# An embedding-attention kernel whose single-row fetches are dealt out anew between ScalarE and SyncE

## The chip, the core and the metric

The kernel runs on one NeuronCore of a Trainium2 chip. Its metric is device microseconds (us) of one execution, the median of three: 16508.57 us before the change (16477.51 to 16532.16). The hardware profiler recorded one execution; its record runs from the first to the last instruction and is called the span.

The engines are named as the profile names them: PE (TensorE, matmuls), PEld (its weight loads), DVE (VectorE), ACT (ScalarE), POOL (GpSimd), SP (SyncE). ACT, SP and POOL also issue DMAs. Each engine works through its own list of instructions in order.

## The reference

The reference scores 16384 users. Each has 69 item numbers and a label; all 70 are looked up in a table of 100001 rows of 96 floats. The 69 looked-up rows pass through a small attention network (one hidden layer of 64), are weighted, summed into 10 groups, and go with the label's row through a top network (200, 80, 1).

```python
u  = emb[batch_user]                    # 16384 x 69 x 96
ql = emb[batch_label[:, 0]]
z  = concatenate([q, u, q - u, q * u])  # q: ql repeated over the 69 fields
h  = _dice(z @ W1 + b1, a1)             # (a*(1-p)+p)*x with p = sigmoid(x)
att = (h @ W2 + b2) @ W3 + b3
pre = where(batch_user < 100000, u * att, 0)
pooled = einsum('gf,bfe->bge', window, pre)
x = concatenate([pooled, ql])
# two dice layers (200, 80), then one output
```

## The kernel before

**Tiling.** 16384 x 69 lookups are 2208 chunks of 512 rows; a chunk is four gathers of 128 rows. Two chunks make a step, so there are 1104 steps. A block is 512 users: 69 chunks, or 34.5 steps; there are 32 blocks. Of a block's 69 chunks, 64 hold eight users with 64 fields each, and the last five hold one field of all 512 users. These five (the tail chunks) take other matmuls, at L396, L401 and L423.

**A step.** `fetch(i)` gathers eight tiles of 128 rows into `u` (POOL, L266), turns each by a PE transpose into `ptr` (L325), and DVE copies it and multiplies it by the label's row (L376, L379). Two steps later `hidden` does the attention layer: PE's matmuls into `ph` (L396 to L403), then on ACT the sigmoid (L405) and, on its result, a scaled identity (L406), and on DVE the product with `ph` (L407): this is the gate. Every fourth step PE turns four gated results into attention scores (`prow`, L414), which ACT copies out (`row`, L416) and DVE spreads into weights (`rw`, L436). Seven steps after the fetch `pool` sums the weighted rows (PE `acc`, L325; DVE, L470). Once per block come the label's gather and its preparation (L348 on PE, copied by ACT at L349) and the top network in ten pieces, with three pairs of activations on ACT (L483, L484).

**Singles.** Some of the 8832 gathers of `u` are not done by POOL. For the chunks that stand in the tables `SP_CHUNKS` and `ACT_CHUNKS` the fourth tile of 128 rows is fetched row by row, by 128 DMAs of 384 bytes (L301) issued from SP or from ACT into a ring of buffers. PE then waits for a semaphore and reads the ring in place of `u`. The byte offset of each row is read from SBUF into a register; one load (L286) brings 32 of them. SP fetches whole tiles; one is needed every 5.5 steps, the table being `2 * (int(5.5 * s) + 6) + 1`. ACT fetches 20 rows in each step, right behind the step's two activations, so a tile takes 6.4 steps; it is needed two steps after its last row. SP's ring has 8 buffers, ACT's 4.

**Order.** The order of the work is written out by hand: a table `plan` has a list of pieces for each step, and the program is emitted step by step. What an engine does when follows from this order and from semaphores alone. The buffers set how far engines may drift apart: `u` has 15 buffers, `ph` 2, `ptr` 2, `acc` 1, `y` 6.

Of the kernel before, what the change touches and what calls it, by code (L numbers as in the profile page):

```python
# [18 lines left out]
P = 128  # L19
# [29 lines left out]

ROW_BYTES = 4 * E  # L50
SLOT = 3
SP_CHUNKS = [2 * (int(5.5 * s) + 6) + 1 for s in range(199)]
SP_RING = 8
ACT_ROWS = 20
ACT_CHUNKS = [2 * ((s + 1) * P // ACT_ROWS + 2) for s in range(170)]
ACT_RING = 4
SINGLES = SP_CHUNKS + ACT_CHUNKS
NSB = (len(SINGLES) + P - 1) // P
NSEM = 8
# [3 lines left out]
def chunk_of(c):  # L63

    n, k = divmod(c, NCH)
    if n == NBLK - 1 and k >= EARLY:
        k = NMAIN + k - EARLY if k < EARLY + NTAIL else k - NTAIL
    return n, k
# [47 lines left out]
def rec_kernel(  # L116
# [269 lines left out]
                nc.vector.tensor_tensor(quT[:, j, :], ptr, q[:, 0:BLK], ALU.mult)  # L386
        return u, uT, quT

    def hidden(i, uT, quT):

        ph = ps_h.tile([P, 512], F32, tag="h", name=f"ph{i}")
        places = [chunk_of(2 * i + j) for j in range(2)]
        sums = [ph[j * H1 : (j + 1) * H1, :] for j in range(2)]
        for (n, k), p in zip(places, sums):
            if k >= NMAIN:
                nc.tensor.matmul(p, Cq, qTs[n % 2], start=True, stop=False)  # L396
        for j, ((n, k), p) in enumerate(zip(places, sums)):
            if k < NMAIN:
                nc.tensor.matmul(p, As[n % 2][:, k // 4, :], uT[j], start=True, stop=False)  # L399
            else:  # L400
                nc.tensor.matmul(p, A, uT[j][0:E], start=False, stop=False)  # L401
        for j, p in enumerate(sums):
            nc.tensor.matmul(p, Wp, quT[:, j, :], start=False, stop=True)  # L403
        y = ypool.tile([P, 512], F32, tag="y", name=f"y{i}")
        nc.scalar.activation(y, ph, AF.Sigmoid, scale=S_DICE)  # L405
        nc.scalar.activation(y, y, AF.Identity, bias=a1c, scale=na1c)  # L406
        nc.vector.tensor_mul(y, ph, y)  # L407
        return y
# [131 lines left out]
    pooled, pres, x1s, x2s, qs, us, hs, ys, bands, rws, p1s = ({} for _ in range(11))  # L540
# [17 lines left out]
    def rows_of(b, n):  # L558
        return lambda: attend_rows(b, n)

    def spread_of(b, n):
        return lambda: spread(b, n)

    def pool_of(k):
        return lambda: pool(k)

    def hidden_of(k):
        return lambda: ys.__setitem__(k, hidden(k, *hs[k]))

    def tails_of(k):  # L570
        def work():
            uT = hs.pop(k)[0]
            for j in range(2):
                if chunk_of(2 * k + j)[1] >= NMAIN:
                    attend_tail(k, j, ys[k], uT)

        return work

    def fetch_of(k, between=()):
        def work():  # L580
            for j in range(2):
                n = chunk_of(2 * k + j)[0]
                if n not in pooled:
                    pooled[n] = bpool.tile([E, G, BLK], F32, tag="pooled", name=f"pooled{n}")
                    pres[n] = xpool.tile([E, NTAIL, BLK], F32, tag="pre", name=f"pre{n}")
            u, uT, quT = fetch(k, lambda: [w() for w in between])
            us[k], hs[k] = u, (uT, quT)

        return work
# [4 lines left out]
    def at(step, *work):  # L594
        plan.setdefault(step, []).extend(work)

    by_sync = Singles("sp", nc.sync, mybir.EngineType.SP, SP_CHUNKS, 0, range(SP_RING), 32)
    for s, m in enumerate(SP_CHUNKS):
        at(max(0, m // 2 - 6), lambda s=s: by_sync.fetch(s, 0, P))

    by_scalar = Singles(
        "act",
# [1 line left out]
        mybir.EngineType.Activation,  # L604
        ACT_CHUNKS,
        len(SP_CHUNKS),
        range(SP_RING, SP_RING + ACT_RING),
        32,
    )
    def scalar_rows(i):  # L610

        row, stop = i * ACT_ROWS, min((i + 1) * ACT_ROWS, len(ACT_CHUNKS) * P)
        while row < stop:
            s, start = divmod(row, P)
            n = min(P - start, stop - row)
            by_scalar.fetch(s, start, start + n)
            row += n

    c = NPAIR - CLOSE
    for i in range(c):  # L620
        if i >= 3 and (i - 3) % 4 == 3:
            at(i, rows_of(i - 6, 4))
        if i >= 3:
            at(i, tails_of(i - 3))
        if i >= 4 and (i - 4) % 4 == 3:
            at(i, spread_of(i - 7, 4))
        if i >= 2:
            at(i, hidden_of(i - 2))
        at(i, lambda i=i: scalar_rows(i))
        if i < c - CLOSE:  # L630
            if i >= POOL_LAG:
                at(i, pool_of(i - POOL_LAG))
        else:

            for k in {0: (-15, -14), 1: (-13,), 3: (-12, -11), 4: (-10, -9), 7: (-8, -7)}.get(i - c + 8, ()):
                at(i, pool_of(c + k))
        at(i, fetch_of(i))

    at(c, pool_of(c - 6), pool_of(c - 5), tails_of(c - 3), hidden_of(c - 2), fetch_of(c))
    at(c + 1, tails_of(c - 2), hidden_of(c - 1), fetch_of(c + 1))  # L640
    at(c + 2, rows_of(c - 4, 4), tails_of(c - 1), hidden_of(c), spread_of(c - 4, 4), pool_of(c - 4), fetch_of(c + 2))
    at(c + 3, pool_of(c - 3), pool_of(c - 2), hidden_of(c + 1), fetch_of(c + 3, [hidden_of(c + 2)]))
# [5 lines left out]
    for n in range(NBLK):  # L648
        first, end = n * NCH // 2, ((n + 1) * NCH - 1) // 2
# [104 lines left out]
```

## Time and profile before

| what | value |
|---|---|
| median of three runs | 16508.57 us |
| span of the profiled execution | 10780.4 us |
| time of the profiled execution itself | not shown; the span lies 5728.2 us below the median of the runs |
| gathers by POOL | 8463 of `u`, 128 of labels |
| rows issued singly by SP and by ACT | 25472 (199 tiles) and 21760 (170 tiles) |
| mean granted PE clock | 0.749 of full speed |

In the groups of instructions, a row reads: line, engine, operation, output<-inputs, shapes, count | busy us, mean ns of one | idle us just before them and what ended it. DMA-issuing instructions on SP and ACT do not count as busy: they stand in the timeline as ACTq and SPq, where a row's second number is the time from the first to the end of the last of a run of equal instructions. An ACT that is idle in the groups may therefore be issuing rows. The record says nothing of what lies outside its first and last instruction.

### The profile page before, as it was taken

Reading aid. Unit: us, or ns where it says so; the run is one execution under the profiler, and the core shown is the slowest. Engines: PE = TensorE matmul, PEld = TensorE weight load, DVE = VectorE, ACT = ScalarE, POOL = GpSimd, SP = SyncE. Lnnn points to the kernel's source line nnn. Section 1 sums busy time; section 2 is a strip of 40 time slices with the busy share of each in tenths; the row PEclk is TensorE's granted clock in tenths of the full one; section 3 lists DMA queues with packets and bytes.
Section 4 is the critical chain, followed back from the end, with each engine's and each line's share of the span. In section 5 each row is a group of like instructions: output and inputs, shape, how many; then the busy total and the mean of one; then the engine's idle time right before and its main releaser. Section 6 shows DMA issues by size and latency. Waiting matters only on the chain.

```text
span 10780.4 us, 204439 instructions
## 1 busy us (share of the span) xinstructions
PE 8756.9 (81%) x41797; PEld 4310.8 (40%) x41797; DVE 4235.1 (39%) x7535; ACT 1884.4 (17%) x2761; POOL 8110.8 (75%) x8597
## 2 busy tenths in 40 slices
PE   6888888888887788877888788888887887888888
PEld 3434444434433344433433344333343343443335
DVE  4333333333333333333333343333333334333333
ACT  1111111111111111111111111111111111111112
POOL 7777777777777777777777777777777777777776
PEclk7777777677777777777777777777777777777778
DMA  2222222222222222222222222222222222222221
GB/s 50 42 42 42 45 42 42 42 42 45 42 42 42 45 42 42 42 42 45 42 42 42 42 44 42 42 42 42 44 42 42 42 42 44 42 42 42 42 42 34
DMA packets 372495, 460.70 MB, mean 43 GB/s; under 512 B 232114, under 2 KB 232626, under 8 KB 371106
## 3 DMA queue, kind: packets, MB, share of 16 engines
q0 software_dynamic: 274912, 422.81, 18.9%
q1 hardware_dynamic: 52802, 16.36, 1.0%
q10 hardware_dynamic: 43520, 8.44, 0.7%
q14 instruction: 925, 7.58, 0.2%
q8 instruction: 336, 5.51, 0.2%
HBM read 446.81 MB, written 0.07 MB: 41 GB/s over the span
## 4 chain that ended last, share of the span: by engine, by line
POOL 40%; PE 21%; issue 19%; DMA 12%; ACTq 6%; ACT 2%; DVE 1%; POOLq 0%
POOL u L266 40%; DMA u<-in_rows,ids 12%; ACTq L301 4%; PE acc L325 4%; PE p L502 4%; PE ph L399 3%; PE ph L403 3%; PE ptr L325 2%; PE prow L414 1%; ACTq L286 1%; PE pa L423 1%; ACT y L405 1%; POOL q L266 1%; PE ph L396 1%; PE ph L401 1%
## 5 line engine op out<-in xcount | busy, mean ns | idle before, releaser
L266 POOL DMA_INDIRECT u<-in_rows,ids x8463 | 7989.1, 944 | 2583.5 <-issue 2389.6
L325 PE MATMUL ptr<-ident,u 128*96 128x128 f32 x8463 | 1925.1, 332 | 1606.1 <-DMA u<-in_rows,ids 1555.6
L407 DVE TENSOR_TENSOR y<-ph,y 128x512 f32<-128x512 f32 x1104 | 763.5, 692 | 4972.6 <-ACT y L406 4699.0
L325 PEld LDWEIGHTS acc<-rw,u 128*96 128x96 f32 x15702 | 1674.4, 188 | 1332.5 <-issue 840.4
L325 PEld LDWEIGHTS ptr<-ident,u 128*96 128x96 f32 x8463 | 1131.6, 151 | 2282.7 <-DMA u<-in_rows,ids 1853.2
L325 PE MATMUL acc<-rw,u 128*96 128x20 f32 x15702 | 1792.0, 259 | 212.0 <-DVE rw L436 177.6
L376 DVE COPY uT<-ptr 96x512 f32<-96x512 f32 x2208 | 1489.0, 674 | 739.9 <-PE ptr L325 737.5
L405 ACT ACTIVATE y<-ph 128x512 f32<-128x512 f32 x1104 | 658.8, 597 | 6119.1 <-PE ph L403 3304.1
L399 PE MATMUL ph<-uT,A 128*64 128x512 f32 x4096 | 1598.9, 856 | 0.0
L403 PE MATMUL ph<-quT,wn 96*64 96x512 f32 x4416 | 1540.5, 767 | 0.0
L379 DVE TENSOR_TENSOR quT<-ptr,qT 96x512 f32<-96x512 f32 x2048 | 1379.1, 673 | 0.0
L406 ACT ACTIVATE y<-y,wn,na1c 128x512 f32<-128x512 f32 x1104 | 897.9, 813 | 36.6
L403 PEld LDWEIGHTS ph<-quT,wn 96*64 96x64 f32 x4416 | 429.4, 183 | 1002.5 <-issue 1001.8
L502 PE MATMUL p<-pooled,wf 96*100 96x512 f32 (+1 forms) x1400 | 667.7, 624 | 0.0
L414 PE MATMUL prow<-y,v 128*32 128x512 f32 x2208 | 507.2, 885 | 65.4 <-DVE y L407 57.6
L399 PEld LDWEIGHTS ph<-uT,A 128*64 128x64 f32 x4096 | 259.6, 172 | 609.6 <-issue 605.5
L416 ACT COPY row<-prow 128x512 f32<-128x512 f32 (+1 forms) x277 | 161.6, 583 | 1733.2 <-issue 675.0
L470 DVE COPY pooled<-acc 96x160 f32<-96x160 f32 x1008 | 420.5, 417 | 99.1 <-PE acc L325 97.6
L502 PE MATMUL p<-pre,V 96*100 96x512 f32 (+1 forms) x700 | 398.0, 714 | 11.1 <-DVE x L485 10.8
L502 PEld LDWEIGHTS p<-pooled,wf 96*100 96x100 f32 x1400 | 249.6, 190 | 316.5 <-issue 316.5
L436 DVE SCALAR_TENSOR_TENSOR rw<-patt,bb,wn 128x320 f32<-128x320 f32 x554 | 276.1, 539 | 116.8 <-PE patt L431 114.7
L485 DVE SCALAR_TENSOR_TENSOR x<-p,wf,g 100x512 f32<-100x512 f32 (+3 forms) x105 | 73.9, 704 | 523.6 <-ACT g L484 523.5
(72 smaller groups left out, 2706.1 us busy)
## 6 DMA issues: line engine op xcount, KB each, us to landing
ring<-in_rows SPq DMA_DIRECT2D x25472, 0.4 KB
ring<-in_rows ACTq DMA_DIRECT2D x21760, 0.4 KB
u<-in_rows,ids POOLq DMA_INDIRECT x8463
ids<-in_idx SPq DMA_DIRECT2D x8, 560.0 KB, 3.9
q<-in_emb,ids POOLq DMA_INDIRECT x128
wf<-in_far SPq DMA_DIRECT2D x1, 1209.0 KB, 8.3
wn<-in_near SPq DMA_DIRECT2D x1, 236.0 KB, 3.4
offsets<-in_single_rows SPq DMA_DIRECT2D x1, 192.0 KB, 2.5
```

Source lines behind the costliest of these rows:

```text
L266: nc.gpsimd.indirect_dma_start(out=dst, out_offset=None, in_=table, in_offset=bass.IndirectOffsetOnAxis(ap=index, axis=0),)
L301: d = self.engine.dma_start(out=ring[r : r + 1, b], in_=row_bytes[:, bass.ds(self.values[r], ROW_BYTES)]).then_inc(self.sems[k], 16)
L325: ins = op(out, ring[:, at[0]].bitcast(F32) if at else u[:, 4 * (c % 2) + t, :], other, **how)
L376: nc.vector.tensor_copy(uT[j][0:E], ptr)
L379: nc.vector.tensor_tensor(quT[:, j, :].rearrange("e (s f) -> e s f", f=FM), ptr.rearrange("e (s f) -> e s f", f=FM), by_field(q[:, k * NS ...
L399: nc.tensor.matmul(p, As[n % 2][:, k // 4, :], uT[j], start=True, stop=False)
L403: nc.tensor.matmul(p, Wp, quT[:, j, :], start=False, stop=True)
L405: nc.scalar.activation(y, ph, AF.Sigmoid, scale=S_DICE)
L406: nc.scalar.activation(y, y, AF.Identity, bias=a1c, scale=na1c)
L407: nc.vector.tensor_mul(y, ph, y)
L414: nc.tensor.matmul(pr[32 * k : 32 * (k + 1), :], v2, ys[b + k], start=True, stop=True)
L502: nc.tensor.matmul(p1, w[:, h * DH : (h + 1) * DH], x, start=(k == 0), stop=(k == KTOP - 1))
```

## The change

Four things are altered, and nothing of what is computed:

- ACT issues 23 rows in a step, not 20; its tiles number 195, not 170, its ring 8 buffers, not 4, and a tile is needed five steps after its last row, not two.
- The first four of a step's 23 rows are issued between the sigmoid and the identity of the gate, the other 19 behind them.
- SP's tiles number 206, not 199, one for every 5.3 steps, not 5.5, and the first is needed at step 8, not 6.
- The table of offsets grows with the number of tiles from three to four times 128 columns.

So 401 tiles are fetched by single rows, not 369, and POOL is left with 8431 gathers of `u`.

```diff
-SP_CHUNKS = [2 * (int(5.5 * s) + 6) + 1 for s in range(199)]
+SP_STEPS = 5.3
+SP_AHEAD = 8
+SP_CHUNKS = [2 * (int(SP_STEPS * s) + SP_AHEAD) + 1 for s in range(206)]
 SP_RING = 8
-ACT_ROWS = 20
-ACT_CHUNKS = [2 * ((s + 1) * P // ACT_ROWS + 2) for s in range(170)]
-ACT_RING = 4
+ACT_ROWS = 23
+ACT_FIRST = 4
+ACT_AHEAD = 5
+ACT_CHUNKS = [2 * ((s + 1) * P // ACT_ROWS + ACT_AHEAD) for s in range(195)]
+ACT_RING = 8
...
         nc.scalar.activation(y, ph, AF.Sigmoid, scale=S_DICE)
+        if between:
+            between()
         nc.scalar.activation(y, y, AF.Identity, bias=a1c, scale=na1c)
...
-        at(max(0, m // 2 - 6), lambda s=s: by_sync.fetch(s, 0, P))
+        at(max(0, m // 2 - SP_AHEAD), lambda s=s: by_sync.fetch(s, 0, P))
...
-    def scalar_rows(i):
+    def scalar_rows(i, first, last):
 
-        row, stop = i * ACT_ROWS, min((i + 1) * ACT_ROWS, len(ACT_CHUNKS) * P)
+        row, stop = (min(i * ACT_ROWS + n, len(ACT_CHUNKS) * P) for n in (first, last))
...
-            at(i, hidden_of(i - 2))
-        at(i, lambda i=i: scalar_rows(i))
+            at(i, hidden_of(i - 2, lambda i=i: scalar_rows(i, 0, ACT_FIRST)))
+        at(i, lambda i=i: scalar_rows(i, ACT_FIRST if i >= 2 else 0, ACT_ROWS))
```

**On ACT**, early in the program; the numbers behind names only tell buffers apart. Before, both activations of a gate stand together and 20 rows follow, with a load of 32 offsets among them where a group begins:

```order
L405 ACTIVATE y_5574<-ph_5569 128x512
L406 ACTIVATE y_5574<-y_5574,wn,na1c 128x512
L301 DMA ring<-in_rows 1x384 x16
L286 TENSOR_LOAD offsets
L301 DMA ring<-in_rows 1x384 x4
L405 ACTIVATE y_5702<-ph_5697 128x512
L406 ACTIVATE y_5702<-y_5702,wn,na1c 128x512
```

Now (the lines carry other numbers: L409 is the sigmoid, L412 the identity, L305 a row, L290 the load):

```order
L409 ACTIVATE y_5722<-ph_5717 128x512
L305 DMA ring<-in_rows 1x384 x4
L412 ACTIVATE y_5722<-y_5722,wn,na1c 128x512
L305 DMA ring<-in_rows 1x384 x15
L290 TENSOR_LOAD offsets
L305 DMA ring<-in_rows 1x384 x4
L409 ACTIVATE y_5853<-ph_5848 128x512
L305 DMA ring<-in_rows 1x384 x4
L412 ACTIVATE y_5853<-y_5853,wn,na1c 128x512
```

Four rows have moved between the two activations, and 19 stand behind them where 20 stood.

**On POOL**, in the first steps, each row below being a step's gathers. Before, where x7 marks a step with one tile left to SP or ACT:

```order
L266 DMA u_1681<-in_rows,ids_79 128x96 x7
L266 DMA u_1762<-in_rows,ids_79 128x96 x8
L266 DMA u_1890<-in_rows,ids_79 128x96 x7
L266 DMA u_2028<-in_rows,ids_79 128x96 x8
L266 DMA u_2098<-in_rows,ids_79 128x96 x8
L266 DMA u_2632<-in_rows,ids_79 128x96 x7
```

Now:

```order
L270 DMA u_1982<-in_rows,ids_79 128x96 x7
L270 DMA u_2123<-in_rows,ids_79 128x96 x8
L270 DMA u_2584<-in_rows,ids_79 128x96 x7
L270 DMA u_2733<-in_rows,ids_79 128x96 x8
L270 DMA u_2864<-in_rows,ids_79 128x96 x8
L270 DMA u_2995<-in_rows,ids_79 128x96 x7
```

Steps with seven gathers begin two steps later (step 8, not 6) and come a little more often over the program; nothing else on POOL has moved.

More of the change, by code (lines that the diff above doesn't have):

```diff
@@ L387, in fetch, with hidden @@
         return u, uT, quT
-    def hidden(i, uT, quT):
+    def hidden(i, uT, quT, between=None):
         ph = ps_h.tile([P, 512], F32, tag="h", name=f"ph{i}")
@@ L565, in pool_of, with hidden_of @@
         return lambda: pool(k)
-    def hidden_of(k):
-        return lambda: ys.__setitem__(k, hidden(k, *hs[k]))
+    def hidden_of(k, between=None):
+        return lambda: ys.__setitem__(k, hidden(k, *hs[k], between))
     def tails_of(k):
```

## The prediction

> **What bounds the kernel now.** I read the page's busy times and its chain of waits first, then the groups by line, the DMA issues, ACT's and PE's timelines in one stretch, and SP's waits.
>
> ```profile
> span 10780.4 us, 204439 instructions
> POOL 40%; PE 21%; issue 19%; DMA 12%; ACTq 6%; ACT 2%; DVE 1%; POOLq 0%
> L266 POOL DMA_INDIRECT u<-in_rows,ids x8463 | 7989.1, 944 | 2583.5 <-issue 2389.6 <-DMA u<-in_rows,ids 79.4 <-PE ptr L325 78.8
> L266 POOL DMA_INDIRECT q<-in_emb,ids x128 | 121.0, 946 | 40.6 <-issue 38.8 <-DMA ids<-in_idx 1.8
> L325 PE MATMUL ptr<-ident,u 128*96 128x128 f32 x8463 | 1925.1, 332 | 1606.1 <-DMA u<-in_rows,ids 1555.6 <-issue 8.2 <-PE ph L403 8.1
> ring<-in_rows SPq DMA_DIRECT2D x25472, 0.4 KB
> ring<-in_rows ACTq DMA_DIRECT2D x21760, 0.4 KB
> ```
>
> POOL is the longest part of the chain. Its 8591 gathers take 7989.1 + 121.0 busy and 2583.5 + 40.6 idle, 10734.2 us together: all of the span but 46.2 us. Nearly all of the idle time is "issue", the gap behind every gather, so POOL waits for nobody. One gather costs 10734.2 / 8591 = 1.2495 us, start to start. PE waits 1606.1 us for gathered rows: without these waits its step would be (10734.2 - 1606.1) / 1104 = 8.27 us, while POOL's is 9.72 us. A block of 34.5 steps takes POOL 10734.2 / 32 = 335.4 us.
>
> How full ACT is the page cannot tell, since issuing rows is not busy time. The timeline can. This is ACT in one stretch (start, length, what; in brackets the idle time of its execution unit):
>
> ```profile
> 5015.05 0.60 ACT L405 ACTIVATE y<-ph 128x512 f32<-128x512 f32 x1 [1.30 <-PE ph L403]
> 5015.68 0.81 ACT L406 ACTIVATE y<-y,wn,na1c 128x512 f32<-128x512 f32 x1
> 5015.75 6.37 ACTq L301 DMA_DIRECT2D ring<-in_rows  x20
> 5022.22 0.60 ACT L405 ACTIVATE y<-ph 128x512 f32<-128x512 f32 x1 [5.72 <-PE ptr L325]
> 5022.85 0.81 ACT L406 ACTIVATE y<-y,wn,na1c 128x512 f32<-128x512 f32 x1
> 5022.92 8.85 ACTq L301 DMA_DIRECT2D ring<-in_rows  x20
> 5031.87 0.60 ACT L405 ACTIVATE y<-ph 128x512 f32<-128x512 f32 x1 [8.20 <-PE ph L403]
> ...
> 5032.56 9.18 ACTq L301 DMA_DIRECT2D ring<-in_rows  x20
> 5044.13 0.60 ACT L405 ACTIVATE y<-ph 128x512 f32<-128x512 f32 x1 [10.82 <-PE ph L403]
> ...
> 5044.83 6.06 ACTq L301 DMA_DIRECT2D ring<-in_rows  x20
> 5050.93 0.58 ACT L416 COPY row<-prow 128x512 f32<-128x512 f32 x1 [5.36 <-PE prow L414]
> 5058.95 0.60 ACT L405 ACTIVATE y<-ph 128x512 f32<-128x512 f32 x1 [7.44 <-PE ph L403]
> ...
> 5059.65 8.92 ACTq L301 DMA_DIRECT2D ring<-in_rows  x20
> 5071.08 0.60 ACT L405 ACTIVATE y<-ph 128x512 f32<-128x512 f32 x1 [10.69 <-PE ph L403]
> ...
> 5097.21 0.58 ACT L416 COPY row<-prow 128x512 f32<-128x512 f32 x1 [7.87 <-issue]
> 5097.69 0.60 ACT L405 ACTIVATE y<-ph 128x512 f32<-128x512 f32 x1
> ```
>
> Two steps in it hold no wait: the rows end 0.10 us before the next sigmoid starts. Without a load of offsets such a step lasts 5022.22 - 5015.05 = 7.17 us; with one, 5031.87 - 5022.22 = 9.65 us. So a load costs 2.48 us, and a row 6.37 / 20 = 0.319 us. Twenty rows need 20/32 of a load per step: 7.17 + 0.625 x 2.48 = 8.72 us, or 300.8 us per block. To this come 8.6 copies of `row` at 0.48 us (5097.21 to 5097.69), 4.1 us, and the top network's pairs:
>
> ```profile
> L484 ACT ACTIVATE g<-g,dice,dice 100x512 f32<-100x512 f32 (+3 forms) x105 | 81.5, 776 | 3.5
> L483 ACT ACTIVATE g<-p,dice 100x512 f32<-100x512 f32 (+3 forms) x105 | 68.1, 649 | 732.7 <-issue 248.8 <-PE p L502 166.2 <-PE ptr L325 131.6
> ```
>
> 3.3 pairs per block hold ACT for the first one's 0.65 us and a start of 0.03, 2.2 us in all. ACT needs 307.1 of a block's 335.4 us and waits the other 28.3: it is 92% full.
>
> **The change part by part.**
>
> *POOL* loses 32 gathers: 32 x 1.2495 = 40.0 us, so its work ends at 10694.2, and a block takes it 334.2 us. The Trainium skill ("Perfetto Trace Analysis", GPSIMD Engine Instruction) says that a GpSimd instruction's reported duration is unreliable and is to be timed start to start; by the reported 944 ns the gain would be 30.2 us, by the spacing 40.0.
>
> *ACT's rows.* Three more rows are 0.96 us. The sigmoid's 0.63 us, in which ACT's queue stood still for the identity, is now covered by the four rows (1.28 us), less 0.07 us to dispatch the identity behind them. A step is 7.17 + 0.96 - 0.63 + 0.07 = 7.57 us, and 23/32 of a load add 1.78: 9.35 us. A block is 322.6 + 4.1 + 2.2 = 328.9 us. That leaves 5.3 us per block under POOL's 334.2, where 28.3 were left before: ACT is 98% full, and what it waits decides.
>
> *Which waits stay.* Most of the 28.3 us arise because ACT has caught up with the gathers; these vanish as it fills. Others come where PE itself is long, and stay. The stretch shows one, at a block's tail chunks. There ACT waited 2.29, 7.44 and 2.41 us (the gaps ahead of the sigmoids at 5044.13, 5058.95 and 5071.08, less the usual 0.10), 12.1 us together. PE in the same stretch:
>
> ```profile
> 5044.02 2.75 PE L325 MATMUL acc<-rw,u 128*96 128x20 f32 x16
> ...
> 5048.45 1.94 PE L414 MATMUL prow<-y,v 128*32 128x512 f32 x8
> 5050.32 3.27 PE L423 MATMUL pa<-y,vrep 64*96 64x512 f32 x4
> 5053.52 1.98 PE L396 MATMUL ph<-qT,Cq 97*64 97x512 f32 x4
> 5055.28 1.92 PE L401 MATMUL ph<-uT,A 96*64 96x512 f32 x4
> 5056.99 1.92 PE L403 MATMUL ph<-quT,wn 96*64 96x512 f32 x4
> ```
>
> PE worked from 5044.02 to 5058.9 almost without a break; no gather was late. ACT cannot start the next sigmoid earlier, and its rows can't run ahead, since they stand behind that sigmoid in its list. Each of the three waits shrinks by the step's growth, 9.35 - 8.72 = 0.63 us: 10.2 us stay. The bounds are 0 (every wait fills up) and 28.3 (every one stays). I take 10.2, for it is the one that a row shows to be PE's own.
>
> *Sum.* An ACT block is then 328.9 + 10.2 = 339.1 us against POOL's 334.2: ACT sets the pace. POOL feels it once `u`'s 15 buffers are used up, that is, once PE is some eight steps behind. ACT's 195 tiles are issued by step 195 x 128 / 23 = 1085, which is 31.45 blocks: 10664.7 us. The 19 steps left run at PE's own pace, 19 x 8.27 = 157 us. With the 46.2 us around POOL's work the span is 10868 us, 87.5 above 10780.4.
>
> *The identity comes later*, by 1.28 - 0.63 = 0.65 us, and by a load's 2.48 more in one step of eight. DVE's product L407 waits for it:
>
> ```profile
> DVE y L407 <- ACT y L406: 4699.0, 1009, 12.3
> ```
>
> Behind the product stand, on DVE, the copies of the next `ptr`. PE needs this `y` only for `prow`, every fourth step, or a step later. As long as ACT keeps up, that covers the delay; with ACT late the cover is thin. Bounds: 0, and 0.65 us in each of the 276 `prow` steps, 180 us. I take 0 and keep half of 180 for the range.
>
> *SP.*
>
> ```profile
> SPq L530 <- DVE r L529: 416.6, 1, 416.6
> SPq L301 <- PE ptr L325: 84.8, 36, 13.2
> ...
> 5000.69 48.89 SPq L301 DMA_DIRECT2D ring<-in_rows  x128
> 5049.95 0.37 SPq L151 DMA_DIRECT2D ids<-in_idx  x1
> 5052.59 57.52 SPq L301 DMA_DIRECT2D ring<-in_rows  x147
> ```
>
> A tile takes SP 5052.59 - 5000.69 - 0.40 = 51.5 us. It had 416.6 us left at the end and waited for a free ring buffer. Now 206 tiles are 10609 us, and the last is needed at step 1094, at POOL's pace 1095 x 9.687 = 10607 us: just in time. At ACT's slower pace (339.1 / 34.5 = 9.83 us per step) it has some 140 us to spare. I cost it at nothing; the cover is ACT's lateness, and without it see the third rival.
>
> *Longer leads and rings* add no instruction; the fourth 128 columns of offsets lengthen one load at the start. Nothing.
>
> **How the span stands to the time.** The runs' median is 5728.2 us above the span, and no view shows what lies there. I take it as unchanged: 16508.57 + 87.5 = 16596 us.
>
> **The rivals.**
>
> 1. *POOL keeps the pace (not slower).* If less than 5.3 us of waits per block stay with ACT, its block fits under 334.2 us and the gain arrives whole: 10740.4 us, and 16468.6. The point from which ACT decides is that block boundary; at 7.4 us of kept waits the change comes out even. For it: 28.3 us per block are unused now, and buffers of eight steps even out a burst of 12 us. Against it: 98% full leaves no way to win back what one late `ph` loses.
> 2. *The 5728 us are the kernel too*, run slower than in the profile. Then the gain of rival 1 scales: 16508.57 x 10740.4 / 10780.4 = 16447 us. Nothing speaks for it but the size of the gap.
> 3. *SP comes late.* Runs of 20 rows on ACT last 6.06 to 6.37 us, 0.016 us per row apart. If ACT's rows and SP's hinder each other by that, 15% more rows on ACT add 0.15 x 128 x 0.016 = 0.3 us to SP's tile; 206 x 51.8 = 10671 us, 64 us after need, and ten steps at 8.27 and the 46.2 follow: some 10800, +20 us, 16528. The Trainium skill ("Perfetto Trace Analysis", DMA Instruction — HWDGE) has the two queues lock one descriptor generator in turn; the spread of ACT's runs is all that this trace shows of it.
>
> **How the numbers follow.** Forecast 0.52, rival 1 0.27, rival 2 0.10, rival 3 0.07; 0.04 for no change of another sort. The forecast's own range is 7 to 14 us of kept waits, 31.45 us of span for each: 16495 to 16715; the identity's delay would lift it further. Of the time before, 0.3% of the time, 49.5 us, is about what a measurement of this kernel tells from no change. Faster: rival 2, and 0.07 of rival 1, whose -0.24% lies near the bound: 0.17. Slower: the forecast without its lowest part, 0.09, which lies under 9 us of kept waits: 0.43. Within: 0.40. The range goes from below rival 1 to near the forecast's upper end, 16455 to 16715; rival 2 and a little above are left out.
>
> **What would show it.** Right: POOL's idle time gains releasers other than issue (PE freeing `u`), and the sum exceeds the present 2624.1 / 8591 = 0.305 us per gather; DVE's wait for the identity grows above its present 4.7 ms, PE's wait for gathers falls, and its waits for `y` and `rw` grow; ACT's rows run on to the next sigmoid almost without gaps, but for the tail chunks. SP's last wait shrinks from 416.6 to some 200 us. Wrong: POOL at 1.2495 us per gather to the end, a span near 10740. It would be wrong by a term if a row in ACT's list costs other than 0.319 us: 0.003 us per row is 2.4 us per block, 75 us in the end.

## The result, and the profile after

| kernel | median of 4 runs, us | lowest to highest |
|---|---|---|
| before, in the same comparison | 16505.62 | 16477.51 to 16532.16 |
| changed | 16778.07 | 16758.14 to 16796.66 |

The ratio is 1.016 (95% interval 1.0142 to 1.0179): slower by 272 us, where 87.5 were forecast.

One thing has to be known ahead of every number below: these programs take very different times on different chips. On two chips the kernel before took 10.78 ms, on the others 16.5 to 16.8 ms, with runs on any one chip within 0.7%. I call them the short and the long chips. Only one of them, a long one, was met in two sets of runs, and it was long both times; nothing else here shows that the difference stays with the chip. On either, a run's time is its span and about 1.8 us. By its span of 10780.4 us the profile that the prediction reads is one of a short chip; the times shown with it are those of a long chip, and so is the result. There were never 5728 us "outside the span".

The page of the changed kernel, on a long chip:

```profile
span 16761.2 us, 212759 instructions
...
SPq 62%; issue 36%; PE 1%; ACTq 1%; DMA 0%; DVE 0%; another core or an unknown queue 0%; ACT 0%; DVEq 0%
...
L270 POOL DMA_INDIRECT u<-in_rows,ids x8431 | 7955.5, 944 | 8546.2 <-PE ptr L329 3572.1
...
L329 PE MATMUL ptr<-ident,ring 128*96 128x128 f32 x401 | 149.6, 373 | 3687.0 <-DMA ring<-in_rows 3592.2
```

The second line is the chain: the work that ended last, followed back from the program's end; "issue" in it is time in which an engine waited for nothing that the profile shows. POOL was 40% of the chain before; here it is absent, and SP's queue has 62%. PE waits 3592.2 us for single tiles in the ring, and POOL, which waited for nobody, now stands idle for 8546.2 us, of which 3572.1 end when PE frees a `u`. SP's own waits:

```profile
SPq L536 <- DVE r L535: 101.8, 1, 101.8
...
SPq L305 <- PE patt L437: 2.0, 8, 0.3
...
SPq L305 <- PE ptr L329: 1.1, 4, 0.3
```

SP waits 3.3 us for a ring buffer in the whole program (the two rows above and one of 0.2 us): it issues rows from end to end. And it is late: PE stands idle for over 0.5 us before 196 of SP's 206 tiles, and before none of ACT's 195 (counted in the trace). What a row costs it is in its timeline, first of the changed kernel on a long chip, then of the kernel before on a short chip (run `before_again`, below):

```profile
8000.03 295.74 SPq L305 DMA_DIRECT2D ring<-in_rows  x481
8296.13 0.37 SPq L155 DMA_DIRECT2D ids<-in_idx  x1
8298.72 301.08 SPq L305 DMA_DIRECT2D ring<-in_rows  x469
```

```profile
5051.32 348.86 SPq L301 DMA_DIRECT2D ring<-in_rows  x873
```

From 8000.03 to 8599.80 SP issued 950 rows, 0.631 us each with their loads of offsets: 80.8 us for a tile of 128. On the short chip it is 348.86 / 873 = 0.400 us, 51.2 us for a tile. 206 tiles x 80.8 = 16645 us, which is all but 116 us of the span.

The chain's 36% "issue" is the time between SP's DMAs and loads, its register moves included. The single records of SP from 8003.48 on (start in ns, ns since the record before, duration, instruction, line) show what slows it; a register move usually takes 29 ns (median):

```
8003482  243   29 MOVE 305
8003540   58  228 DMA_DIRECT2D 305
8004033  493  700 MOVE 305
8004741  708   22 DMA_DIRECT2D 305
8004776   35 1387 MOVE 305
8006178 1402    4 DMA_DIRECT2D 305
8006195   17  709 MOVE 305
8007593 1398   13 DMA_DIRECT2D 305
8007611   18  707 MOVE 305
8008332  721  689 DMA_DIRECT2D 305
8009024  692   13 MOVE 305
8009041   17   13 DMA_DIRECT2D 305
8009063   22   29 MOVE 305
8009121   58  227 DMA_DIRECT2D 305
```

For 5.5 us instructions go through in steps of 0.7 us or twice that, moves as well as DMAs; then they run on at their usual 0.32 us per row. I call SP held wherever 0.45 to 1.6 us pass from the start of one of its row instructions (a move or a DMA) to its next record. By this count, over all records of the changed kernel, SP is held for 55% of the span, and 5947 of its moves and DMAs take over 0.6 us. In the kernel before on a short chip it is held for 1.1%, and none takes that long.

The holds follow POOL's gathers in time. SP is held for 72% of the time up to 1.25 us from the start of a gather, for 95% of the time from 1.25 to 2.5 us behind one, and for 28% from 2.5 to 4 us. Of the 3750 us in which the last gather started longer ago than that, it is held for 1.5%. When gathers begin again after more than 4 us without one (410 times), SP is held for 3% of the first microsecond and for 89% of the sixth. This says that holds come and go with gathers on a long chip; on the short one POOL gathers almost without a pause, and SP is hardly ever held.

### The profile page after: what moved, and what is told of

Its sections match the earlier page's. It is cut to its first block, busy times and chain, and to the rows that moved or that the text cites. A ratio compares the mean times of both kernels' runs of the same rounds, so it can differ in the third digit from the quotient of the medians.

```text
span 16761.2 us, 212759 instructions
## 1 busy us (share of the span) xinstructions
PE 9024.3 (54%) x41797; PEld 4667.1 (28%) x41797; DVE 4188.3 (25%) x7535; ACT 1879.8 (11%) x2761; POOL 8077.2 (48%) x8565
## 4 chain that ended last, share of the span: by engine, by line
SPq 62%; issue 36%; PE 1%; ACTq 1%; DMA 0%; DVE 0%; another core or an unknown queue 0%; ACT 0%; DVEq 0%
SPq L305 53%; SPq L290 9%; ACTq L305 0%; PE p L508 0%; PE acc L329 0%; DMA ring<-in_rows 0%; PE ptr L329 0%; PE ph L403 0%; PE ph L407 0%; ACTq L290 0%; PE patt L437 0%; PE prow L420 0%; ACT y L412 0%; DVE uT L380 0%
## 5 line engine op out<-in xcount | busy, mean ns | idle before, releaser
L270 POOL DMA_INDIRECT u<-in_rows,ids x8431 | 7955.5, 944 | 8546.2 <-PE ptr L329 3572.1
L329 PE MATMUL acc<-rw,u 128*96 128x20 f32 x15636 | 1968.2, 272 | 1516.5 <-issue 663.8
L329 PEld LDWEIGHTS acc<-rw,u 128*96 128x96 f32 x15636 | 1846.4, 205 | 2635.1 <-issue 1513.8
L329 PE MATMUL ptr<-ident,ring 128*96 128x128 f32 x401 | 149.6, 373 | 3687.0 <-DMA ring<-in_rows 3592.2
L329 PE MATMUL ptr<-ident,u 128*96 128x128 f32 x8431 | 1553.7, 336 | 403.5 <-issue 319.1
L409 ACT ACTIVATE y<-ph 128x512 f32<-128x512 f32 x1104 | 659.1, 597 | 9159.6 <-issue 4227.4
L329 PEld LDWEIGHTS ptr<-ident,u 128*96 128x96 f32 x8431 | 1219.2, 165 | 558.5 <-issue 482.2
L420 PE MATMUL prow<-y,v 128*32 128x512 f32 x2208 | 712.1, 849 | 1032.2 <-issue 610.4
L329 PEld LDWEIGHTS ptr<-ident,ring 128*96 128x96 f32 x401 | 62.1, 155 | 3752.0 <-issue 3398.6
L412 ACT ACTIVATE y<-y,wn,na1c 128x512 f32<-128x512 f32 x1104 | 897.4, 813 | 1271.2 <-issue 1007.6
L420 PEld LDWEIGHTS prow<-y,v 128*32 128x32 f32 x2208 | 82.1, 126 | 1359.2 <-issue 857.0
```

Source lines behind the costliest of these rows:

```text
L270: nc.gpsimd.indirect_dma_start(out=dst, out_offset=None, in_=table, in_offset=bass.IndirectOffsetOnAxis(ap=index, axis=0),)
L329: ins = op(out, ring[:, at[0]].bitcast(F32) if at else u[:, 4 * (c % 2) + t, :], other, **how)
L420: nc.tensor.matmul(pr[32 * k : 32 * (k + 1), :], v2, ys[b + k], start=True, stop=True)
```

## The experiments

The kernels were run in five sets, each on one chip with the kernel before beside it, and ratios are against that. The chip could not be chosen: three sets fell on long chips (two of them on the same one), two on short ones. The theories named in the expectations are: S, single rows set the pace by what they cost their issuer; O, the 5728 us lie outside the program; A, ACT sets the pace (the forecast); E, single rows overload the DMA queues, so that POOL's gathers come late.

### The kernel before once more, and with hardly any single rows (short chip)

`before_again` is the kernel before, unaltered.

> The kernel before, unchanged, for a second profile of it. Theory S (SyncE's rows set the pace of the timed runs; they are lengthened while POOL gathers, as in the changed kernel's record, where the chain that ended last is SPq 62% and issue 36%): the span is near 16500 us, not 10780; SP's 199 tiles take about 16500/199 = 83 us each where the first record had 51.5; SP's wait for the last output is about 100 us, and PE waits for ring rows in thousands of us. Rival O (the 5728 us between the first record and the runs lie outside the program): the span is again near 10780 and the time near 16500.

Measured: 10781.31 us, ratio 1.000 (0.999 to 1.0011), and 10781.83 for the profiled run, whose span is 10780.1. Theory O falls: 1.7 us lie between span and time.

```diff
-SP_CHUNKS = [2 * (int(5.5 * s) + 6) + 1 for s in range(199)]
+SP_CHUNKS = [2 * (int(5.5 * s) + 6) + 1 for s in range(4)]
-ACT_CHUNKS = [2 * ((s + 1) * P // ACT_ROWS + 2) for s in range(170)]
+ACT_CHUNKS = [2 * ((s + 1) * P // ACT_ROWS + 2) for s in range(4)]
```

> The kernel before with 4 single-row tiles on SP and 4 on ACT in place of 199 and 170; POOL makes 8952 gathers. Theory S: nothing but POOL is left to set the pace, 8952 x 1.2495 + 46 = 11232 us, two thirds of before. Rival O: 11232 + 5728 = 16960 us, ratio 1.027.

Measured: 11219.47 us, ratio 1.0408 (1.0391 to 1.0426). On a short chip POOL sets the pace of the kernel before, as the prediction read it: 361 gathers more cost 438 us, 1.21 us each. The Trainium skill ("Perfetto Trace Analysis", GPSIMD Engine Instruction) says to time GpSimd from start to start; the run agrees, since 361 times the reported 944 ns would be 341 us and 361 times 1.2495 are 451.

### The two halves of the change (short chip)

SP's half:

```diff
-SP_CHUNKS = [2 * (int(5.5 * s) + 6) + 1 for s in range(199)]
+SP_CHUNKS = [2 * (int(5.3 * s) + 8) + 1 for s in range(206)]
-        at(max(0, m // 2 - 6), lambda s=s: by_sync.fetch(s, 0, P))
+        at(max(0, m // 2 - 8), lambda s=s: by_sync.fetch(s, 0, P))
```

> The kernel before with SP's part of the change alone: 206 tiles, one per 5.3 steps, needed from step 8; ACT as before. Theory S: seven more tiles cost between SP's own 51.5 us and its whole 83 us each, +360 to +580 us, ratio 1.022 to 1.035. Rival A (ACT sets the pace, as predicted): no more work on ACT, seven gathers fewer, ratio 0.999 to 1.001.

Measured: 10774.58 us, ratio 0.9995 (0.9986 to 1.0005). SP's half costs nothing here, and seven gathers fewer (8.7 us) account for the 6.6 us gained, which are within what the runs can tell from none.

ACT's half is the change with SP's table as before (199 tiles, one per 5.5 steps, six ahead).

> ACT's part of the change alone: 23 rows a step, four of them between the gate's two activations, 195 tiles, lead 5, ring 8; SP as before. Theory S: SP's 199 tiles stay, POOL has 25 gathers fewer to disturb it, ratio 0.995 to 1.003. Rival A: the whole loss of the change stands here, ratio 1.010 to 1.020.

Measured: 11121.25 us, ratio 1.0316 (1.0299 to 1.0333): 340 us lost. Queues, chain and groups on the page of this run, and then the same of `before_again`:

```profile
span 11118.5 us, 210937 instructions
...
q1 hardware_dynamic: 52802, 16.42, 2.5%
q10 hardware_dynamic: 49920, 9.68, 2.1%
...
DMA 31%; ACTq 21%; POOL 19%; PE 14%; issue 13%; ACT 1%; DVE 1%; POOLq 0%
...
L270 POOL DMA_INDIRECT u<-in_rows,ids x8438 | 7964.5, 944 | 2950.7 <-issue 2220.4
```

```profile
q1 hardware_dynamic: 52802, 16.36, 1.1%
q10 hardware_dynamic: 43520, 8.44, 0.7%
...
POOL 41%; PE 20%; issue 19%; DMA 11%; ACTq 6%; ACT 1%; DVE 1%; POOLq 0%
...
L266 POOL DMA_INDIRECT u<-in_rows,ids x8463 | 7990.2, 944 | 2583.4 <-issue 2404.3
```

Releasers of POOL's gathers (us, times, longest), in the same order:

```profile
POOL u L270 <- DMA u<-in_rows,ids: 589.3, 972, 2.6
POOL u L270 <- PE ptr L329: 82.9, 160, 2.5
```

```profile
POOL u L266 <- PE ptr L325: 76.3, 250, 0.3
POOL u L266 <- DMA u<-in_rows,ids: 71.4, 234, 0.3
```

POOL is idle 367 us longer; less the 26 us of the 25 gathers that it no longer makes, that is the whole loss. What released it is an earlier gather of its own, 589.3 us against 71.4, while its waits for PE hardly grew (82.9 against 76.3). In 504 of its 616 waits of over 0.5 us, by the trace, it was the landing of the gather eight before; in `before_again` a single wait of POOL is that long. No wait is longer than 2.6 us, so POOL was never stopped for long by a lack of `u` buffers. The packets of SP's and ACT's queues take 4.6% of the DMA engines' time where they took 1.8%, though there are only 7% more of them. So here gathers land late, as theory E has it, and the wait that the forecast's A needs is not there. That the slower row packets are what makes them late is argued from these shares, not shown by a run of its own. ACT's queue too has grown, from 6% of the chain to 21%.

### The parts on a long chip

`after_again` is the changed kernel unaltered. `rows_behind` is ACT's half without the split (all 23 rows behind the identity). `between_only` has 20 rows, four of them between the activations, with lead (the steps between a tile's last row and its use) and ring as before. `lead_ring` alters lead and ring, and has one tile less:

```diff
-ACT_CHUNKS = [2 * ((s + 1) * P // ACT_ROWS + 2) for s in range(170)]
-ACT_RING = 4
+ACT_CHUNKS = [2 * ((s + 1) * P // ACT_ROWS + 5) for s in range(169)]
+ACT_RING = 8
```

> The changed kernel, unchanged, beside runs of the one before in which POOL keeps its pace (10781 us). Theory E (the single-row DMAs all run on one of the 16 DMA engines; with the denser rows it falls behind, a gather's share on it lands late, and POOL waits for that): like ACT's part alone, 11100 to 11250 us, ratio 1.030 to 1.045, and POOL's long waits are for gathers, none over 5 us. Theory A (ACT sets the pace, the forecast): 11000 to 11200, with POOL waiting for PE to free u, in gaps over 5 us.

> ACT's part of the change with all 23 rows behind the second activation (lead 5, ring 8, 195 tiles). Theory A: a step costs ACT 0.56 us more than with four between, 0.56 x 1085 = 600 us: ratio 1.07 to 1.09. Theory E: the same rows reach the DMA engine at a slower rate if anything: 1.01 to 1.03, not above ACT's part alone (1.0316).

> The kernel before with four of its 20 rows issued between the two activations, lead 2 and ring 4 as before. Theory A: ACT gains 0.56 us a step, POOL goes on setting the pace, ratio 0.999 to 1.001. Theory E: the rows are as many as before; 0.999 to 1.001, unless it is their bunching that fills the DMA engine, then 1.01 or more.

> The kernel before with ACT's lead of 5 steps and ring of 8 buffers alone (20 rows a step behind the activations, 169 tiles). Theories A and E: POOL has one gather more, ratio 1.000. If it is the ring's place or size in SBUF that makes a row's write longer (median 22 ns before, 173 ns with ACT's part), 1.01 or more, with that longer write.

These four expectations were written for a short chip. The runs met a long one, where SP is last, so they cannot decide between A and E as worded.

In the next set, on another long chip, SP's half (`sp_alone`, the edit of `sp_part`) ran beside repeats of two of them; the second repeats ran on that chip too, in the set after it:

> SyncE's part of the change alone: 206 tiles, one per 5.3 steps, eight steps ahead. Where the kernel before takes about 16.76 ms: if SyncE's rows set the pace, 7 tiles x 51.4 us less 0.57 x 7 gathers x 1.2495 = +355 us, 17119, a ratio of 1.021, and the whole loss of the change; if the change loses there by ScalarE, 1.000. Where the kernel before takes 10.78 ms: 0.9995, as this kernel had there.

| kernel | us | ratio to before, in the same set (95%) |
|---|---|---|
| `after_again` | 17027.84 | 1.0164 (1.0146 to 1.0182) |
| `sp_alone` | 17094.01 | 1.0178 (1.0152 to 1.0205) |
| `rows_behind`, repeated as `rows_behind_again` and `rows_third` | 16672.78, 16669.14, 16646.57 | 0.9955, 0.9933, 0.9938 (0.9908 to 0.9971 over all) |
| `between_only`, repeated as `between_again` and `between_third` | 16777.31, 16794.19, 16764.16 | 1.0012, 1.0009, 1.0009 (0.9995 to 1.0023 over all) |
| `lead_ring` | 16773.43 | 1.0005 (0.9996 to 1.0015) |

SP's half alone loses 325 us, more than the whole change (263 in this table, on the other chip). Seven tiles were expected to cost 355. ACT's part without the split gives back 92 to 100 us; why so much, with SP still last (62% of the chain in `rows_third`), is open. The split, at 20 rows, and the longer lead and ring are at most 0.2%. ACT's half with the split was not run alone on a long chip; by difference (263 against 325) it gains some 60 us. On a long chip the change is slower because SP, which is last there, gets more to do.

### Taking rows away from the slow side (long chip)

Half of SP's tiles, first alone, then with half of ACT's:

```diff
-SP_CHUNKS = [2 * (int(5.5 * s) + 6) + 1 for s in range(199)]
+SP_CHUNKS = [2 * (11 * s + 6) + 1 for s in range(99)]
```

> SyncE carries 99 tiles, one per 11 steps, in place of 199; ScalarE keeps 170, and GpSimd makes 100 gathers more (8691). Where the kernel before takes about 16.76 ms: if SyncE's rows set the pace there (a tile costs SyncE 51.4 us of its own, and it loses about 0.57 of the time in which GpSimd gathers), SyncE needs 99 x 51.4 + 0.57 x 8691 x 1.2495 = 11279 us and GpSimd about 10860 + 46, so 11280 to 11500, a ratio of 0.67 to 0.69. If something else makes that program long (what theory O said, time outside the program), 16764 + 125 = 16889. Where the kernel before takes 10.78 ms, GpSimd sets the pace: 10781 + 100 x 1.2495 = 10906, a ratio of 1.012; less, down to 10850, if single rows delay its gathers in the DMA queues.

Measured: 14562.1 us, ratio 0.8675 (0.8648 to 0.8703). SP's theory gave 11280 to 11500. The first half of it holds: with 99 tiles SP is off the chain. The second doesn't: ACT's rows are last now.

```profile
ACTq 49%; issue 29%; PE 13%; ACT 6%; another core or an unknown queue 2%; DVE 2%; POOL 0%; DMA 0%; DVEq 0%
```

```diff
+SP_CHUNKS = [2 * (11 * s + 6) + 1 for s in range(99)]
-ACT_ROWS = 20
-ACT_CHUNKS = [2 * ((s + 1) * P // ACT_ROWS + 2) for s in range(170)]
+ACT_ROWS = 10
+ACT_CHUNKS = [2 * ((s + 1) * P // ACT_ROWS + 2) for s in range(84)]
```

> SyncE carries 99 tiles (one per 11 steps) and ScalarE 84 (ten rows per step), so GpSimd makes 186 gathers more than before (8777). Where the kernel before takes about 16.76 ms: if the rows of both engines are what is held there (with 99 tiles on SyncE alone the chain went over to ScalarE's rows and the time to 14562), both are now short enough for GpSimd to set the pace, 8777 x 1.2495 + 46 = 11013, up to 11600 where rows still come late now and then; a ratio of 0.66 to 0.69. If the loss there is not in the rows, 14562 or more. Where before takes 10.78 ms: GpSimd's 11013, a ratio of 1.0215, less 2 us per hundred tiles taken from the DMA queues at most.

And `few_again`, the kernel `few_singles` on a long chip:

> Four single tiles on each of SyncE and ScalarE, as in the run few_singles; GpSimd makes 8952 gathers. Where the kernel before takes about 16.76 ms: if that time is made by the rows alone, 8952 x 1.2495 + 46 = 11232, the same as the 11219 where before takes 10.78 ms, a ratio of 0.67; if GpSimd itself, PE or the DMA engines are slower there too, clearly more than 11232. Where before takes 10.78 ms: 1.041, as this kernel had there.

Measured: `half_both` 13553.24 us, ratio 0.8094 (0.808 to 0.8107); `few_again` 13540.68, ratio 0.8084 (0.807 to 0.8098). Both gain 19%, and both stop at the same 13.55 ms, far above POOL's 11.0 and 11.2. So the rows of SP and ACT are some six tenths of what a long chip loses: of 16744 - 10781 = 5963 us, 13541 - 11219 = 2322 stay with `few_again`. There PE has 48% of the chain. The first view is a stretch of PE's timeline in `few_again`, the second the same kernel on a short chip:

```profile
6006.00 1.07 PE L325 MATMUL ptr<-ident,u 128*96 128x128 f32 x4
6007.72 0.37 PE L325 MATMUL ptr<-ident,u 128*96 128x128 f32 x1 [0.65 <-issue]
6009.82 0.37 PE L325 MATMUL ptr<-ident,u 128*96 128x128 f32 x1 [1.73 <-issue]
6011.92 0.37 PE L325 MATMUL ptr<-ident,u 128*96 128x128 f32 x1 [1.73 <-issue]
6014.72 0.37 PE L325 MATMUL ptr<-ident,u 128*96 128x128 f32 x1 [2.42 <-issue]
```

```profile
6005.89 0.42 PE L325 MATMUL ptr<-ident,u 128*96 128x128 f32 x1 [0.86 <-DMA u<-in_rows,ids]
6007.13 0.45 PE L325 MATMUL ptr<-ident,u 128*96 128x128 f32 x1 [0.81 <-DMA u<-in_rows,ids]
6008.31 0.45 PE L325 MATMUL ptr<-ident,u 128*96 128x128 f32 x1 [0.74 <-DMA u<-in_rows,ids]
```

On the short chip a transpose follows each gather, 1.2 us apart, and waits for the gather. On the long one transposes stand 2.1 to 2.8 us apart, three and four steps of 0.7 us, and wait for nothing the profile shows. PE's own list is held in the same steps as SP's. Its waits of that kind for `ptr`, and POOL's for PE in turn, are in the waits of `few_again`; on the short chip POOL's longest wait for PE is 0.3 us:

```profile
POOL u L266 <- PE ptr L325: 1127.3, 247, 61.5
...
PE ptr L325 <- issue: 1072.6, 842, 51.9
```

POOL's wait for these transposes is half of the 2226 us by which it stands idle longer before its gathers of `u` than on the short chip (4914.8 against 2689.2); 989.5 us of the rest were ended by something that the profile does not name.

### Gathers left out, and all rows behind the identity (short chip)

To see whether the gathers hold the other engines, `half_gathers` leaves two of a chunk's four out: the second and third tile read the first one's rows, so that its result is another one.

```diff
-ring[:, at[0]].bitcast(F32) if at else u[:, 4 * (c % 2) + t, :]
+ring[:, at[0]].bitcast(F32) if at else u[:, 4 * (c % 2) + (t if t == SLOT else 0), :]
-                else:
+                elif t in (0, SLOT):
```

> The kernel before with two of GpSimd's gathers left out of each chunk of four (the second and the third tile read the first one's rows), so 4111 gathers in place of 8591 and another result; SyncE's 199 and ScalarE's 170 tiles stay. Where the kernel before takes about 16.76 ms: if the gathers are what holds SyncE's instructions, 51.4 x 199 + 0.57 x 4111 x 1.2495 = 13156, a ratio of 0.785, and SyncE still sets the pace; if a tile of SyncE just costs some 83 us on that chip whatever GpSimd does, 16500, a ratio of 0.98 to 1.00. Where before takes 10.78 ms: GpSimd no longer sets the pace; SyncE's 199 x 51.4 = 10229 or PE's 9100 us busy do, so 10230 to 10500, a ratio of 0.95 to 0.975.

`rows_fourth` is `rows_behind`, which had not met a short chip till then:

> ScalarE's 23 rows, all behind the identity, 195 tiles, lead 5, ring of 8. Where the kernel before takes 10.78 ms: if the number of rows (15% more per step) is what makes one DMA engine fall behind, near 11121, a ratio of 1.03, with row packets of over 100 ns in the mean on ScalarE's and SyncE's queues; if the four rows between the activations are, packets of some 45 ns and 10750 (0.997) with GpSimd at its pace, or 10868 (1.008) if ScalarE's instructions set it, as forecast. Where before takes 16.76 ms: 0.9933 to 0.9955, as this kernel had there.

Measured: `half_gathers` 10351.45 us, ratio 0.9603 (0.9587 to 0.9619). Both kernels met a short chip, so no run shows whether a long one is held less when gathers are taken away. It does show how near the next limit is: with POOL relieved of half its work, SP sets the pace only 4% lower, at (10347.8 - 118.7 of its last wait) / 199 = 51.4 us per tile:

```profile
SPq 54%; issue 16%; ACTq 16%; PE 10%; ACT 3%; DVE 1%; DMA 1%
```

```profile
SPq L530 <- DVE r L529: 118.7, 1, 118.7
```

`rows_fourth` took 11410.7 us, ratio 1.0585 (1.0567 to 1.0602). This is not what either branch of its expectation gave: the split is not the cause of the loss, it lessens it, from 629 us to 340 (on two short chips, where the kernel before agrees within 0.01%). Chain and POOL's releasers:

```profile
ACTq 60%; issue 15%; PE 11%; ACT 8%; DMA 4%; POOL 2%; DVE 1%; POOLq 0%
```

```profile
POOL u L270 <- PE ptr L329: 398.5, 263, 10.2
POOL u L270 <- DMA u<-in_rows,ids: 293.5, 555, 2.9
POOL u L270 <- PE acc L329: 170.2, 71, 10.9
```

ACT in one stretch:

```profile
5007.79 9.88 ACTq L305 DMA_DIRECT2D ring<-in_rows  x23
5017.77 0.60 ACT L409 ACTIVATE y<-ph 128x512 f32<-128x512 f32 x1 [9.24 <-PE ph L407]
5018.40 0.81 ACT L412 ACTIVATE y<-y,wn,na1c 128x512 f32<-128x512 f32 x1
5018.47 7.28 ACTq L305 DMA_DIRECT2D ring<-in_rows  x23
5025.84 0.60 ACT L409 ACTIVATE y<-ph 128x512 f32<-128x512 f32 x1 [6.63 <-PE ptr L329]
5026.47 0.81 ACT L412 ACTIVATE y<-y,wn,na1c 128x512 f32<-128x512 f32 x1
5026.54 10.04 ACTq L305 DMA_DIRECT2D ring<-in_rows  x23
```

This is the forecast's theory A: rows end 0.1 us before the next sigmoid, step after step; ACT's queue has 60% of the chain, and POOL waits up to 10.9 us for PE to free a `u`. Here the DMA queues are the lesser part (293.5 us).

## Why the prediction was right in its sign, by luck, and wrong in its size

**The time outside the span.** The prediction says "no view shows what lies there" and "I take it as unchanged": this step failed, and the result with it. The 5728.2 us are the kernel on a chip on which SP, not POOL, ends last. Rival 2 named the premise (the kernel itself, run slower) and drew the wrong conclusion: it scaled POOL's gain. A longer run need not have the same bound, and here it had another. So the forecast of "slower" came true by luck: where it was measured, SP's tiles cost the time, and ACT's half, which was to cost it, gained some by the difference above.

**SP costed at nothing.** On a short chip this is right (`sp_part`, 0.9995). On a long one it is the term that decides: the prediction's 51.5 us per tile are 80.8 there, seven more tiles cost 325 us, and no lateness of ACT covers them. Rival 3 had the place (SP late) and a wrong price, 0.3 us per tile where 29.3 were to be added. The room that the prediction gave SP at ACT's pace is also a little off by its own figures, 1095 x 9.83 - 10609 = 155 us and not 140; nothing hung on it. SP's last wait did shrink, to 101.8 us, but `lead_ring`, with SP as before, has as little on a long chip, so this sign told nothing:

```profile
SPq L530 <- DVE r L529: 109.3, 1, 109.3
```

**POOL's 40 us.** Its price per gather holds on a short chip (`few_singles`). The gain did not come, since POOL set the pace in no kernel with 23 rows, on neither kind of chip.

**ACT sets the pace.** For a short chip the mechanism is right and shown in `rows_fourth`. By the prediction's own terms that kernel, without the split, has steps of 7.17 + 0.96 + 1.78 = 9.91 us, blocks of 341.9 + 4.1 + 2.2 + 10.2 = 358.4, and a span of 31.45 x 358.4 + 157 + 46.2 = 11475; measured 11409.8, that is 8.1 us of kept waits per block instead of 10.2. For `act_part`, with the split, the same sum gave 10868, and 11118.5 came: by this sum (11118.5 - 203.2) / 31.45 - 328.9 = 18.2 us per block are lost beside ACT's own work where 10.2 were taken, within the bounds of 0 and 28.3. What they are made of was not forecast: by what released POOL, they are gathers that land late, and not PE's length at the tail chunks. The split was worth 289 us, where the prediction's 0.63 - 0.07 us per step would give 607.

**The identity's delay** was put at 0, up to 180 us. On long chips rows between the activations cost 13 to 25 us in three runs (ratios of 0.9995 to 1.0023, so hardly told from none); alone on a short chip they were not run. **Longer leads and rings** cost nothing, as said (1.0005).

**The signs to look for.** POOL's idle time has other releasers than issue, as was said for ACT's sake; on the long chip it is SP that makes PE late, so the sign was right for another reason. DVE's wait for the identity did not grow from 4699.0 us but fell, since ACT wasn't the engine that was late:

```profile
DVE y L413 <- ACT y L412: 3667.0, 431, 66.5
```

No kernel here beats the one before on both kinds of chip: `few_singles` is 4.1% slower on the short one and 19% faster on the long one. The whole change was not run on a short chip; its ACT half alone loses 3.2% there.

## What to carry to other kernels

Where the profiled span and the timed runs differ by a third, the first question is which of them the profile describes; a bound read from one need not be the bound of the other, and no gain may be carried over unseen. An engine that is 90% full of small issues is a bound in waiting: price its list per instruction and ask what happens if that price rises by half. Work moved off a limiting engine onto engines that are 92 to 98% full only pays while each of them keeps its price.

## What the runs showed of the hardware that was not expected

- The same program took 10.78 ms on two chips and 16.5 to 16.8 ms on others; why is open. The granted PE clock isn't the cause: the two runs of the kernel with few singles have 0.728 (11217.0 us) and 0.721 (13528.7 us).
- On the long chips instructions of SP, ACT and PE go through in steps of 0.7 us, register moves too. In the changed kernel 5947 moves and DMAs of SP and 4193 of ACT take over 0.6 us, on a short chip none; on SP such stretches last 6 us in the mean. On SP they set in some microseconds after gathers begin and are gone 4 us after the last one started (held for 1.5% of the time beyond that, against 95% shortly before). That the gathers cause them is likely by this order in time, but not shown: no run on a long chip left gathers out. What is physically held stays open.
- On a short chip 15% more rows on ACT bring the packets of SP's and ACT's queues from 1.8% of the DMA engines' time to 2.9% (rows behind the identity) and 4.6% (four of them ahead of it, a shorter program). The median packet of 384 bytes takes 22 ns in the kernel before and with the rows behind the identity, and 173 to 174 ns with the split. Why the split makes packets slower is open; the record doesn't say which DMA engine carries a packet.
